# Cross-attention by block products: VectorE's sums woven, three more block products in fresh banks, one product of the result in blocks

## The chip, the cores and the metric

The kernel runs on one core of a Trainium2 chip. The metric is the time of one execution in device microseconds. Everything is in float32.

## The reference

For each of 8 batches, with x1 and x2 of 512 channels by 1024 places:

```
q = einsum("bcn,dc->bnd", x1, Wq) + bq            # 1024 x 64
k = einsum("bcn,dc->bdn", x2, Wk) + bk[:, None]   # 64 x 1024
v = einsum("bcn,dc->bdn", x2, Wv) + bv[:, None]   # 512 x 1024
attn = softmax(einsum("bnd,bdm->bnm", q, k), axis=2)
out  = einsum("bcm,bnm->bcn", v, attn) + x1
```

The kernel doesn't form v. It computes y = x2 times the transposed attention first (512 x 1024 by 1024 x 1024), and then the result as Wv times y, plus bv and x1.

## The kernel before

**Two large products, each by seven smaller ones.** Both y = x2 * e (e: the exponentials of the scores) and result = Wv * y are cut into 2 x 2 blocks and computed by a scheme of seven products in place of eight. `MULT` names for each product 1 to 7 its left and right operand and the bank in which it accumulates. Left operands are blocks 11, 12, 21, 22 and the sums S1 to S4; right operands blocks 11 to 22 and T1 to T4. The sums are made by VectorE (`left_sums`, `right_sums`, `sum_y`), by ScalarE, or by DMAs that accumulate (`add_11`, `sum_t3`, `sum_t4`). "Product 5 of y" and "product 7 of the result" below are these products; in the code the stages are "y" (`first`) and "o" (`second`).

**Blocks within a product.** A product of y is 256 x 512 by 512 x 512. Computed plainly (`multiply`, L365) it is eight matmuls of 128 x 128 by 128 x 512. It can be cut once more by the same scheme of seven: its left sums come from `inner_left`, its right sums from `inner_right`, and `inner_product` (L442) issues two matmuls of 256 columns per block product. Three small accumulators are used: `chain`, `third` and the banks of the product itself. ScalarE copies `chain` into the banks between the block products (L479), and VectorE adds `third` at the end (`complete`, L485). `multiply_seeded` does this in a fresh bank; `multiply_onto` does it on a bank that holds a sum already, with the parts that the chain gives in a tile `d` (L451), which VectorE adds later.

Before the change, products 1, 2, 7 and 3 of y are seeded in batches 1 to 7, product 4 goes onto bank c, product 5 goes onto bank a in batches 1 to 5 (`multiply_5`) and is plain in batches 6 and 7, and product 6 is plain. All seven products of the result are plain.

**Banks.** PSUM has eight banks of 512 columns: a0, a1, c0, c1 and two double ones (`sc`). The scores of one half (four tiles) use `sc` for three tiles and a pair of the others for one: c in half 0, a in half 1 (`scores_and`). `chain` and `third` take `sc` too.

**Order.** The instructions of each engine stand in the order in which the code emits them (`tc.manual_schedule`). `period(s, n, nn, nnn)` emits one batch s together with work for the next ones: the scores of batch n in halves 0 and 1, maxima (`fold`, `highest`), exponentials (`lower` on VectorE, `exponential` on ScalarE), sums of the exponentials (`total`), queries and keys of nn, and the loads of nnn. A batch runs on TensorE in this order: products 1, 2, 6 of y, scores of half 0, queries, products 5, 7, 3, scores of half 1, keys, product 4; then products 1, 6, 2, 5, 7, 3, 4 of the result. Batch 0 has an order of its own. In the last batch product 3 of the result comes last, and `evict_o("12")` writes out its halves.

**Names in the rows.** `yT L542` is `evict_t3`, `y L556` is `evict_y`, `y L547` is `scale_y`, `e L293` is `lower`, `e L297` the exponential, `max L248` and `sum L248` are folds, `aI L418` the left sums of blocks, `eI... L431, L434, L435` the right sums, `uy L524` and `d L531` the additions of `multiply_4` and `multiply_5`, `o`, `uo`, `x_in_x_dram L579 to L612` the eviction of the result. `den<-row` spreads a half's shares (one over the sum) over the partitions.

Of the kernel before, what the change touches and what calls it, by code (L numbers as in the profile page):

```python
# [15 lines left out]
def kernel(  # L16
# [195 lines left out]
    def scores(s, h, i, bank=None):  # L212
# [19 lines left out]
        def copy():  # L232
            if bank:
                for g in range(2):
                    nc.scalar.copy(e[:, g, i, :], ps[g])
            else:
                nc.scalar.copy(e[:, :, i, :], whole)  # L237
# [4 lines left out]
    def fold(s, h, i, kind, op):  # L242

        e = s.e[h]
        if i == 1:
            s.mx[h] = sb.tile([P, 2, H], F32, tag="fold", name=f"{kind}_{s.b}_{h}", bufs=2)
        f = s.mx[h]
        nc.vector.tensor_tensor(f, e[:, :, 0, :] if i == 1 else f, e[:, :, i, :], op)  # L248

# [44 lines left out]

    def exponential(s, h, i):
        e = s.e[h][:, :, i, :]
        nc.scalar.activation(e, e, AF.Exp)  # L297
# [39 lines left out]
    def sum_e(s, *ks, of=(0, 2)):  # L337
        for i in of:
            part = {n: v[:, i : i + 2, :] for n, v in s.t.items()}
            for k in ks:  # L340
                right_sums(part, k)

    def sum_y(s, k):
# [5 lines left out]
        else:  # L349
            nc.vector.tensor_tensor(y[k], y["22" if k == "T1" else "21"], y["T2"], ALU.subtract)  # L350

# [13 lines left out]
    def multiply(s, stage, i, left, right, n_k, last=False, hook=None):  # L365
# [4 lines left out]
        if stage == "o" and i == 2:  # L370
            bank, opens = "p", False
        for j in range(2):
# [22 lines left out]
    def multiply_o1(s):  # L395

        for j in range(2):
# [5 lines left out]
            s.bank["a", j] = a = ps_a.tile([P, H], F32, tag=f"a{j}", name=f"ps_oa{j}_{s.b}_1")  # L403
# [8 lines left out]
    def inner_left(s, i, x, tag):  # L412

        v = {f"{p + 1}{q + 1}": x[:, ts(q, MH // 2), ts(p, P)] for p in range(2) for q in range(2)}
        sums = sb.tile([P, 4, MH // 2, P], F32, tag=tag, name=f"aI{i}_{s.b}")
        for z, (k, x, y, op) in enumerate(LEFT):
            v[k] = sums[:, z]
            nc.vector.tensor_tensor(v[k], v[x], v[y], op)  # L418
        s.inner[i] = v

    def inner_right(s, i, x, *tags):

        v = {
            f"{q + 1}{r + 1}": x[:, ts(q, MH // 2), ts(r, H // 2)] for q in range(2) for r in range(2)
        }
        last = 4 // len(tags)
        shape = [P, last, MH // 2, H // 2]
# [5 lines left out]
        )  # L433
        nc.vector.tensor_tensor(t2, both[:, 0], v["22"], ALU.subtract)  # L434
        nc.vector.tensor_tensor(t4, v["21"], t2, ALU.add)  # L435
        s.inner[i, "t"] = v | {"T1": both[:, 0], "T3": both[:, 1], "T2": t2, "T4": t4}

    def inner_product(s, i, z, ps, opens, *copies):

        ka, kb, _, _ = MULT[z]  # L440
        for k in range(MH // 2):
# [5 lines left out]
                stop=z in (2, 3, 4) and k == MH // 2 - 1,  # L447
# [11 lines left out]
    def multiply_seeded(s, i, v_tag, hooks={}):  # L459

        bank = MULT[i][2]
        b0, b1 = (
            ps_a.tile([P, H], F32, tag=f"{bank}{j}", name=f"ps_y{bank}{j}_{s.b}_{i}") for j in range(2)
        )
        s.bank[bank, 0], s.bank[bank, 1] = b0, b1
        chain, third = inner_parts(s, i)
        v = sb.tile([P, 2, H], F32, tag=v_tag, name=f"v{i}_{s.b}")[:, 0, left]
        for z, ps, opens, out, of in (
            (1, chain, True, b0[:, left], chain),
            (7, third, True, v, third),  # L470
            (6, chain, False, b1[:, left], chain),
            (2, b0[:, left], False, None, None),
            (5, chain, False, b0[:, right], chain),
            (4, b1[:, left], False, b1[:, right], chain),
            (3, b0[:, right], False, None, None),
        ):
# [3 lines left out]
            if z in hooks:  # L480
                hooks[z]()

# [37 lines left out]
    def multiply_4(s, hooks={}):  # L520

        d, complete = multiply_onto(s, 4, "u5" if s.b < B - 1 else "a21", "r", hooks)
# [3 lines left out]
    def multiply_5(s, hooks):  # L526

        d, complete = multiply_onto(s, 5, "u5", "r", hooks)
        complete()
        for j in range(2):  # L530
            nc.vector.tensor_tensor(d[:, j, :], s.bank["a", j], d[:, j, :], ALU.add)  # L531
        s.tmp[5] = d
# [6 lines left out]
    def evict_t3(s):  # L539
        s.y["T3"] = y = sb.tile([P, 2, H], F32, tag="y12", name=f"yT3_{s.b}")  # L540
        for j in range(2):
            nc.vector.tensor_tensor(y[:, j, :], s.bank["a", j], s.tmp[7][:, j, :], ALU.add)  # L542
# [24 lines left out]
    def evict_o(s, k):  # L567


        bank, add = RESULT[k] if k != "11" else ("p", None)  # L570
        r, h = int(k[0]) - 1, int(k[1]) - 1
# [192 lines left out]
    def period(s, n, nn, nnn):  # L764
# [4 lines left out]
        def first(i):  # L769
            multiply(s, "y", i, s.a, s.t, MH)  # L770
# [19 lines left out]
        def scores_0():  # L790
            then = scores_and(n, 0, 1, "c", next_queries if nn else nothing)
# [14 lines left out]
        if n is None:  # L806
            load_x(s, x1)
# [33 lines left out]
        else:  # L841
# [10 lines left out]
            if n:  # L852
                sum_t3(s, 0)
                sum_t3(s, 2)
            complete_2()
            evict_y(s, "11")
            if n is None:
                sum_e(s, "T3")
            sum_t4(s)
            first(6)  # L860
            inner_left(s, 7, s.a["S3"], "yT4")
            if five:
                inner_left(s, 5, s.a["S1"], "i2")
                inner_right(s, 5, s.t["T1"], "y21", "u1")
            sum_a(s, "S4")
            if n:
                evict_q = scores_0()
            spread(s, 0)
            shares(s, 1)
# [152 lines left out]
```

## Time and profile before

| | |
|---|---|
| median of 3 runs | 682.23 us (681.3 to 682.25) |
| span of the profiled execution, first to last instruction | 680.8 us |
| TensorE busy | 672.1 us (99%) |
| weight loads, beside the matmuls | 397.9 us (58%) |
| VectorE busy | 615.2 us (90%) |
| ScalarE busy | 336.9 us (49%) |
| GpSimd busy | 218.5 us (32%) |
| DMA | 131.09 MB, 193 GB/s on the mean |
| batch 2, from 205.23 to 287.25 us | TensorE busy 82.02 of 82.02 us |

The page gives no time of the profiled execution beside its span; the three times lie 0.5 to 1.45 us above that span. A busy TensorE is one whose modelled matmul times touch each other. Rows of a timeline give the start in us from the span's start, the time in us, engine, line, operation, what is written from what, the count, and in brackets the idle time ahead with what ended it.

### The profile page before, as it was taken

What the parts mean: (1) busy time and instruction counts of PE and PEld (TensorE: products, weight loads), DVE (VectorE), ACT (ScalarE), POOL (GpSimd) and SP (SyncE); (2) the same over time, 40 slices, a digit from 0 to 9 for tenths busy, and PEclk for the clock granted to TensorE, in tenths of its full rate; (3) what the DMA queues carried; (4) which work ended last, traced back from release to release, by engine and by line L of the source; (5) the groups of instructions that cost most, each with busy time, mean ns of one, the idle gap of its engine ahead of it and who ended that gap; (6) DMA issues with size and microseconds to landing.
All of it is one profiled execution on the core that took longest, in us unless ns stands there. A gap on an engine that the chain in (4) does not pass through costs nothing.

```text
span 680.8 us, 7209 instructions
## 1 busy us (share of the span) xinstructions
PE 672.1 (99%) x2420; PEld 397.9 (58%) x2420; DVE 615.2 (90%) x763; ACT 336.9 (49%) x564; POOL 218.5 (32%) x182
## 2 busy tenths in 40 slices
PE   8999999999999999999999999999999999999997
PEld 5333554757547565566656576464854747556763
DVE  1999998899999999999999998999989979999884
ACT  2734266365554564544644637446475356553320
POOL 0124215251153502643125421344213451154100
PEclk9999999999999999999999999999999999999999
DMA  9656658967798759969499693996947985489503
GB/s 300 271 191 241 155 212 139 240 138 246 180 249 221 154 202 253 214 185 245 123 297 199 174 264 116 280 212 160 277 89 174 222 194 110 92 146 268 144 13 110
DMA packets 50772, 131.09 MB, mean 193 GB/s; under 512 B 5552, under 2 KB 7856, under 8 KB 50736
## 3 DMA queue, kind: packets, MB, share of 16 engines
q0 software_dynamic: 22464, 54.60, 44.7%
q1 hardware_dynamic: 27984, 75.64, 30.8%
q10 hardware_dynamic: 288, 0.39, 0.2%
q8 instruction: 19, 0.31, 0.2%
q14 instruction: 17, 0.14, 0.1%
HBM read 87.30 MB, written 16.81 MB: 153 GB/s over the span
## 4 chain that ended last, share of the span: by engine, by line
PE 84%; DVE 6%; DMA 5%; issue 2%; ACT 1%; SPq 1%; POOL 1%; DVEq 0%; POOLq 0%; ACTq 0%
PE ps_ya L380 11%; PE ps_oa L380 11%; PE ps_yc L442 8%; PE ps_oc L380 7%; PE ps_ya L442 6%; PE ps_s L228 5%; PE ps_o L400 4%; PE ps_o L380 4%; PE ps_k L181 3%; PE ps_q L181 3%; PE ps_i4chain L442 3%; PE ps_i3chain L442 3%; PE ps_i7chain L442 2%; PE ps_i1chain L442 2%; PE ps_i2chain L442 2%
## 5 line engine op out<-in xcount | busy, mean ns | idle before, releaser
L263 POOL PARTITION_ALL_REDUCE den<-sum x16 | 52.6, 3285 | 97.4 <-DVE few L271 60.3
L258 POOL PARTITION_ALL_REDUCE top<-max x16 | 37.6, 2352 | 126.3 <-DVE max L252 75.7
L380 PE MATMUL ps_ya<-eT,aS 128*128 128x512 f32 x176 | 77.5, 594 | 0.0
L293 DVE TENSOR_TENSOR e<-e,top 128x1024 f32<-128x1024 f32 x60 | 69.9, 1218 | 0.0
L620 POOL DMA_DIRECT2D sum<-e x21 | 32.1, 1530 | 108.7 <-ACT sum L625 42.0
L297 ACT ACTIVATE e<-e 128x1024 f32<-128x1024 f32 x60 | 61.8, 1058 | 4.7 <-DVE e L293 4.0
L380 PE MATMUL ps_oa<-yT,w_S 128*128 128x512 f32 x128 | 57.5, 592 | 0.0
L380 PE MATMUL ps_oc<-yT,w 128*128 128x512 f32 x128 | 57.4, 592 | 0.0
L380 PEld LDWEIGHTS ps_ya<-eT,aS 128*128 128x128 f32 x176 | 33.2, 190 | 40.1 <-issue 37.9
L237 ACT COPY e<-ps_s 128x1024 f32<-128x1024 f32 x46 | 45.6, 1032 | 9.0 <-PE ps_s L228 8.8
L228 PE MATMUL ps_s<-q,k 64*128 64x512 f32 x188 | 47.9, 608 | 0.9 <-ACT q L647 0.8
L380 PEld LDWEIGHTS ps_oa<-yT,w_S 128*128 128x128 f32 x128 | 24.3, 190 | 30.6 <-issue 30.6
L380 PEld LDWEIGHTS ps_oc<-yT,w 128*128 128x128 f32 x128 | 24.3, 190 | 30.6 <-issue 29.2
L248 DVE TENSOR_TENSOR max<-max,e 128x1024 f32<-128x1024 f32 x30 | 36.7, 1225 | 2.2
L391 ACT COPY uo<-ps_oa 128x512 f32<-128x512 f32 x32 | 18.7, 586 | 34.9 <-PE ps_oa L380 34.9
L391 ACT COPY uy<-ps_ya 128x512 f32<-128x512 f32 x24 | 13.9, 588 | 36.8 <-PE ps_ya L380 36.8
L228 PEld LDWEIGHTS ps_s<-q,k 64*128 64x128 f32 x188 | 17.1, 186 | 24.5 <-issue 18.0
L479 ACT COPY ps_ya<-ps_i1chain 128x256 f32<-128x256 f32 x28 | 10.0, 357 | 42.2 <-PE ps_i1chain L442 38.7
L547 DVE TENSOR_TENSOR y<-y,den 128x1024 f32<-128x1024 f32 x24 | 29.3, 1221 | 0.3
L418 DVE TENSOR_TENSOR aI<-a 128x256 f32<-128x256 f32 x58 | 29.4, 547 | 0.0
L380 PE MATMUL ps_oa<-y,w_S 128*128 128x512 f32 (+1 forms) x68 | 28.8, 567 | 0.0
L400 PE MATMUL ps_o<-y,w 128*128 128x512 f32 x64 | 28.8, 592 | 0.0
(202 smaller groups left out, 1539.0 us busy)
## 6 DMA issues: line engine op xcount, KB each, us to landing
x_in_x_dram<-in_x_dram SPq DMA_DIRECT2D x60, 512.0 KB, 7.6
a<-in_x2T_dram SPq DMA_DIRECT2D x32, 512.0 KB, 10.1
sum<-e POOLq DMA_DIRECT2D x21, 512.0 KB, 10.1
aS<-in_x2T_dram POOLq DMA_DIRECT2D x14, 512.0 KB, 8.9
uo<-in_x_dram POOLq DMA_DIRECT2D x14, 512.0 KB, 9.9
r<-in_x_dram POOLq DMA_DIRECT2D x14, 512.0 KB, 12.2
out_dram<-r SPq DMA_DIRECT2D x14, 512.0 KB, 6.5
eT<-eT POOLq DMA_DIRECT2D x14, 512.0 KB, 10.1
```

Of the source, the lines that this page charges most:

```text
L181: nc.tensor.matmul(ps[r, :], w_sb[:, c, :], s.x[:, c, ts(h, H)], start=(c == 0), stop=(c == CT - 1),)
L228: nc.tensor.matmul(ps[g], s.k[r, ts(i, P)], s.q[r, ts(h, H)], start=True, stop=True)
L237: nc.scalar.copy(e[:, :, i, :], whole)
L248: nc.vector.tensor_tensor(f, e[:, :, 0, :] if i == 1 else f, e[:, :, i, :], op)
L258: nc.gpsimd.partition_all_reduce(s.top[h], s.mx[h][:, 0, :], P, ReduceOp.max)
L263: nc.gpsimd.partition_all_reduce(s.den[h], s.mx[h][:, 0, :], P, ReduceOp.add)
L293: nc.vector.tensor_tensor(e, e, top, ALU.subtract)
L297: nc.scalar.activation(e, e, AF.Exp)
L380: nc.tensor.matmul(ps[:, n], left[ka][:, k, ts(j, P)], right[kb][:, k, n], start=opens and k == 0, stop=i in (2, 3, 4) and k == n_k - 1, s ...
L391: nc.scalar.copy(s.tmp[i][:, j, :], ps)
L400: nc.tensor.matmul(ps, w["11"][:, k, ts(j, P)], s.y["11"][:, k, :], start=k == 0, stop=False, skip_group_check=True)
L442: nc.tensor.matmul(ps, s.inner[i][ka][:, k, :], s.inner[i, "t"][kb][:, k, :], start=opens and k == 0, stop=z in (2, 3, 4) and k == MH // 2 ...
```

## The change

- **Products 3, 4 and 5 of y in fresh banks.** In batches 1 to 7 product 3 is seeded in bank c, product 4 in bank c (a in the last batch), and product 5 in bank a. y22 is then product 5 plus u6 plus product 7, so `join_67` adds the copy of product 7 to that of product 6, and y22 and y21 are evicted with it. `multiply_5` goes; `multiply_4` stays for batch 0.
- **Product 5 in blocks in batches 6 and 7 too.**
- **Product 7 of the result in blocks**, batches 1 to 7 (`multiply_57`): seven block products of one matmul of 256 columns each, with pieces of products 5 and 3 between them, so that product 3 comes ahead of product 4. Its left sums are made once, in batch 0 (`left_values`); its right sums from T3 of y in each batch. In the last batch half of product 3 (`rest`) still comes last. `o_bank` swaps banks a and c in the last batch.
- **VectorE's sums woven**: `inner_left` and `inner_right` become streams, and `weave` takes an instruction of each in turn. Left sums of 7 with the folds of the sum, left and right sums of 5, right sums of 7 with left sums of 3, right sums of 3 with a `lower`, left and right sums of 4, right sums of 1 with left sums of 2, and others.
- **Order.** In batches 1 to 5 the maxima of half 1 come ahead of the completion of product 4, and the last part of half 0's sum (`add_tile(n, 0, 3)`) and S3's (`add_11`) ahead of product 1 of the result. In the last batch T3 is made by ScalarE and a DMA, and the shares' reciprocals come later. In batch 6 the scores of half 0 come between the two halves of product 6, and those of half 1 are copied in another order. The last batch's x1 is loaded in batch 6.

```diff
+    def join_67(s):
+        nc.vector.tensor_tensor(s.tmp[6], s.tmp[6], s.tmp[7], ALU.add)
...
     def sum_e(s, *ks):
+        order = [(k, i) for i in (0, 2) for k in ks]
+        for k, i in order if s.b == 0 else sorted(order):
+            right_sums({n: v[:, i : i + 2, :] for n, v in s.t.items()}, k)
...
+    def weave(*streams):
+        streams = list(streams)
+        while streams:
+            for stream in list(streams):
+                if next(stream, "end") == "end":
+                    streams.remove(stream)
...
+    def multiply_57(s):
+        s.inner["o7"] = inner_w["o7"]
+        on, fresh = o_bank(s, "a"), o_bank(s, "c")
...
+        chain, third = inner_parts(s, "o7")
...
+        plain(5, 0, 0, 1)
+        inner_product(s, "o7", 1, chain, True, b0[:, left])
+        inner_product(s, "o7", 7, third, True, v)
+        plain(5, 1, 0)
+        inner_product(s, "o7", 6, chain, False, b1[:, left])
+        inner_product(s, "o7", 2, b0[:, left], False)
+        plain(5, 1, 1)
+        inner_product(s, "o7", 5, chain, False, b0[:, right])
+        inner_product(s, "o7", 4, b1[:, left], False)
+        nc.scalar.copy(b1[:, right], chain)
+        plain(3, 0, 0)
+        inner_product(s, "o7", 3, b0[:, right], False)
+        plain(3, 0, 1)
+        if s.b < B - 1:
+            plain(3, 1, 0, 1)
...
     def evict_t3(s):
-            nc.vector.tensor_tensor(y[:, j, :], s.bank["a", j], s.tmp[7][:, j, :], ALU.add)
+            nc.vector.tensor_tensor(
+                y[:, j, :], s.bank["c" if s.b else "a", j], s.tmp[7][:, j, :], ALU.add
+            )
...
     def evict_y(s, k):
         bank, add = RESULT[k]
+        if s.b and k == "22" or s.b == B - 1 and k == "21":
+            bank, add = "a", 6
...
     def scores_0():
-            then = scores_and(n, 0, 1, "c", next_queries if nn else nothing)
+            then = scores_and(n, 0, 1 if nn else 2, "c", next_queries if nn else nothing)
+            if nn is None:
+                first(6, (1,))
...
-            for i in range(1, MH):
-                fold(s, 1, i, "sum", ALU.add)
-            total(s, 1)
-            invert(s, 0)
+            sums_5 = left_stream(s, 5, s.a["S1"], "i2"), right_stream(s, 5, s.t["T1"], "y21", "u1")
+            if n:
+                weave(folds(s, 1, "sum", ALU.add), left_stream(s, 7, s.a["S3"], "yT4"))
+                total(s, 1)
+                invert(s, 0)
+            else:
+                weave(folds(s, 1, "sum", ALU.add), left_stream(s, 7, s.a["S3"], "yT4"))
+                weave(*sums_5)
...
-            if five:
-                multiply_5(s, {6: evict_q})
+            complete_5 = multiply_seeded(
+                s, 5, "r", {6: evict_q} if five else {}, "a"
+            )
+            complete_5()
             if n is None:
-                sum_e(s, "T3")
...
+                shares(s, 1)
...
-            hooks = {2: lambda: copy_7(s, 0), 5: lambda: copy_7(s, 1)}
+            hooks = {7: lambda: copy_7(s, 1)}
...
-            complete_3 = multiply_seeded(s, 3, "r", hooks)
+            copy_7(s, 0)
+            if n:
+                lower(n, 0, 1)
+            complete_3 = multiply_seeded(s, 3, "r", hooks, "c")
...
+            join_67(s)
+            evict_y(s, "22")
...
+            if n:
+                for i in range(2, MH):
+                    lower(n, 0, i)
             complete_3()
             evict_t3(s)
...
+            if nn is None:
+                load_x(n, x1)
...
+        if five:
+            weave(folds(n, 1, "max", ALU.max))
...
-        multiply_4(s, hooks)
+        if s.b == 0:
+            multiply_4(s, hooks)
+        else:
+            complete_4 = multiply_seeded(s, 4, "r", hooks, "c" if n else "a")
+            if five:
+                highest(n, 1)
+            complete_4()
...
         evict_y(s, "21")
+        if n is None:
+            sum_y(s, "T1")
+        if five:
+            add_tile(n, 0, 3)
+            add_11(n, "S3")
         scale_y(s, "21")
...
+        if five:
+            weave(iter_t4(s), right_stream(s, "o7", s.y["T3"], "eT1"))
...
-        second(5)
+        if late:
+            complete_7, rest = multiply_57(s)
+        else:
+            second(5)
...
-            second(3)
+            if s.b == 0:
+                second(3)
             evict_o(s, "12")
             second(4)
             total(n, 0)
...
         else:
             second(4)
             evict_o(s, "21")
-            second(3)
+            rest()
             evict_o(s, "12")
```

More of the change, by code (lines that the diff above doesn't have):

```diff
@@ L248, in fold, with folds @@
         nc.vector.tensor_tensor(f, e[:, :, 0, :] if i == 1 else f, e[:, :, i, :], op)
+    def folds(s, h, kind, op):
+        for i in range(1, MH):
+            fold(s, h, i, kind, op)
+            yield
     def fold_halves(s, h, op):
```

232 lines of the change are left out of this document (147 added, 85 removed).

## The prediction

> **What bounds the kernel now.** I read the page first, then busy time by stretch, then the waits of TensorE, the chain in order of time, and each engine's timeline over batch 2, which stands for batches 2 to 5.
>
> ```profile
> span 680.8 us, 7209 instructions
> ...
> PE 672.1 (99%) x2420; PEld 397.9 (58%) x2420; DVE 615.2 (90%) x763; ACT 336.9 (49%) x564; POOL 218.5 (32%) x182
> ```
>
> ```profile
> core 0: us, PE busy (x) PEld busy (x) DVE busy (x) ACT busy (x) POOL busy (x), PEclk, DMA share, GB/s
> ...
> 205.23:287.25 82.02, 82.02 (x306) 50.52 (x305) 77.71 (x98) 43.83 (x74) 28.99 (x24) 1.00 0.84 209
> ...
> 533.40:609.80 76.40, 76.11 (x262) 46.03 (x261) 70.75 (x87) 41.49 (x68) 28.93 (x24) 1.00 0.69 146
> 609.80:680.80 71.00, 67.19 (x229) 43.01 (x227) 55.07 (x73) 18.71 (x41) 11.61 (x10) 1.00 0.50 137
> ```
>
> The first row of stretches is batch 2: TensorE is busy for all 82.02 us at clock 1.00. The other two are batches 6 and 7, where VectorE is idle for 5.65 and 15.9 us. TensorE's price list stands in the chain; each matmul leaves two records, so x16 is eight matmuls.
>
> ```profile
> 194.07 3.43 PE ps_oc L380 x8
> ...
> 205.23 0.86 PE ps_i1third L442 x4
> ...
> 216.46 6.87 PE ps_ya L380 x16
> ```
>
> A plain product of y is eight matmuls of 512 columns, 6.87 us; a plain product of the result four, 3.43; one block product of y is two of 256 columns, 0.86, so 0.43 each. Two rows of TensorE's timeline bracket product 3 of y and one half's scores in batch 2:
>
> ```profile
> 242.66 1.03 PE L442 MATMUL ps_i3chain<-e,aS 128*128 128x256 f32 x4
> ...
> 252.48 3.65 PE L181 MATMUL ps_k<-x_in_x_dram,wqk_sb 128*64 128x512 f32 x16
> ```
>
> A product of y in blocks is 7 x 0.863 = 6.04 us, so one half's scores take 252.48 - 242.66 - 6.04 = 3.8, and a projection 3.6. Batch 2 has six products of y in blocks (36.2), one plain (6.9), seven plain ones of the result (24.0), two sets of scores and two projections (14.8): 81.9 of its 82.02 us are matmul slots. TensorE has no slack there, and a matmul less is time less, unless a new wait comes.
>
> **The change part by part.** My sum goes against the span of 680.8. The three times shown lie 0.5 to 1.45 us above it; their median, 682.23, is 1.4 above, and I carry that over.
>
> *Product 7 of the result in blocks, batches 1 to 7.* Four matmuls of 512 columns become seven of 256: 3.43 - 7 x 0.43 = 0.41 us; seven times, 2.9 us.
>
> *Product 5 of y in blocks in batches 6 and 7* (1 to 5 had it): 6.87 - 7 x 0.863 = 0.83 us, twice, 1.7 us. VectorE gets some 4.3 us more of sums in each; the idle 5.65 and 15.9 us of those two rows cover it. Without that cover batch 6 alone would lose what its product saves.
>
> *Products 3, 4 and 5 in fresh banks.* TensorE does the same here. What goes is a wait:
>
> ```profile
> PE ps_sa L228 <- DVE yT L542: 0.9, 1, 0.9
> ...
> PE ps_i4third L442 <- ACT e L237: 0.3, 1, 0.3
> ```
>
> ```profile
> 158.92 1.03 PE L442 MATMUL ps_i3chain<-e,aS 128*128 128x256 f32 x4
> ...
> 167.94 1.29 PE L228 MATMUL ps_sa<-q,k 64*128 64x512 f32 x3 [0.89 <-DVE yT L542]
> ...
> 170.44 1.94 PE L181 MATMUL ps_k<-x_in_x_dram,wqk_sb 128*64 128x512 f32 x8
> ```
>
> From product 3 to the keys takes 170.44 - 158.92 = 11.52 us in batch 1 and 252.48 - 242.66 = 9.82 in batch 2. In batch 1 the scores' third tile needs bank a, which evict_t3 (L542) still reads. Now product 3 lies in c, and bank a holds product 5, which VectorE evicts (y22) ahead of evict_t3. So 1.7 us goes. The other wait in the view, 0.3 in batch 6, is for a copy of the scores; I leave it. Next late after the one that goes would be y22: by the walk below it is evicted 5.4 us after product 3's start, and the tile comes some 8 us after it (6.04 of product 3 and two tiles of scores).
>
> *The weaving.* VectorE is the next engine, so its spacing decides whether these savings stand.
>
> ```profile
> 216.12 2.49 DVE L248 TENSOR_TENSOR sum<-sum,e 128x1024 f32<-128x1024 f32 x2
> ...
> 245.24 3.49 DVE L293 TENSOR_TENSOR e<-e,top 128x1024 f32<-128x1024 f32 x3
> 250.44 0.75 DVE L418 TENSOR_TENSOR aI<-a 128x256 f32<-128x256 f32 x2
> ...
> 271.53 1.59 DVE L418 TENSOR_TENSOR aI<-a 128x256 f32<-128x256 f32 x2
> ```
>
> Three independent instructions of 1024 take 3.49 us: they start (3.49 - 1.22) / 2 = 1.13 apart. Two of which the second needs the first take 2.49, so 1.25 apart. Putting another stream's instruction in between saves about 0.12 us per dependence; the woven pairs break some twenty in a batch, 2.4 us. [...]
>
> ```profile
> L524 DVE TENSOR_TENSOR uy<-uy,d 128x1024 f32<-128x1024 f32 x8 | 10.5, 1314 | 0.3
> L485 DVE TENSOR_TENSOR ps_yc<-ps_yc,v 128x512 f32<-128x512 f32 x14 | 9.6, 684 | 0.7 <-ACT ps_yc L479 0.7
> L531 DVE TENSOR_TENSOR d<-ps_ya,d 128x512 f32<-128x512 f32 x10 | 6.4, 682 | 0.0
> L418 DVE TENSOR_TENSOR aI<-a,aI 128x256 f32<-128x256 f32 x58 | 24.6, 425 | 2.0
> ```
>
> Against it stand, per batch: right sums of result product 7 (one of 512, 0.69; two of 256, 0.85) and its completion (0.69) added, 2.2 us; the two L531 additions gone, 1.3; L524's 1.31 replaced by join_67, some 1.25. VectorE's net is 0.9 - 2.4, or 1.5 us less. The four left sums of the weights, once in batch 0, cost 1.6; VectorE waits for half 0's sum there anyway.
>
> *The new order around product 4, batches 1 to 5.* Half 1's maxima (three folds, one of halves, and their all-reduce on POOL) now stand ahead of product 4's completion on VectorE. Queued behind them are y21's eviction and scaling, and TensorE's product 2 of the result waits for that.
>
> ```profile
> 244.59 0.37 ACT L479 COPY v<-ps_i3third 128x256 f32<-128x256 f32 x1 [0.51 <-PE ps_i3third L442]
> ```
>
> ```profile
> 261.37 0.69 DVE L516 TENSOR_TENSOR d<-d,v 128x512 f32<-128x512 f32 x1 [0.87 <-ACT d L451]
> ...
> 263.42 1.29 DVE L556 TENSOR_TENSOR y<-ps_yc,uy 128x512 f32<-128x512 f32 x2
> 264.75 1.23 DVE L547 TENSOR_TENSOR y<-y,den 128x1024 f32<-128x1024 f32 x1
> ```
>
> ```profile
> 269.08 3.60 PE L380 MATMUL ps_o<-y,w 128*128 128x512 f32 x8
> ```
>
> The walk on batch 2's clock: product 7's second copy follows ScalarE's row at 244.59 and ends near 245.5. VectorE's join_67 waits for it. Then join 1.3, y22 1.2, two lowerings 2.3, product 3's completion 0.6, T3 1.2, the woven sums of 4 3.7, three scalings 3.4, T2 1.1, three folds 3.7, halves 0.6: 264.7, where the old completion stood at 261.37. Completion 0.6, y21 1.3, scaling 1.2: ready at 267.9, and product 2 starts at 269.08. 1.2 us are left, so I cost this at nothing. Each us beyond them costs up to 5 us over the five batches. A stretch as in the row at 271.53 (1.59 for 0.75, beside the maximum's all-reduce) would take 0.84. In return half 0's last sum starts earlier on POOL.
>
> *Product 7's blocks amid 5 and 3.* With one slab, a block lasts 0.43 us, so ScalarE's copies must be quick.
>
> ```profile
> 205.33 0.36 ACT L479 COPY ps_ya<-ps_i1chain 128x256 f32<-128x256 f32 x1 [3.66 <-PE ps_i1chain L442]
> ```
>
> That copy is for a block that, by the chain, ended at about 205.07: it starts 0.26 later and lasts 0.36, 0.62 in all. In the new order a block and a piece of product 5 or 3 (0.43 + 0.86 = 1.29 us) lie between a block and whoever needs its copy. 0.6 us spare: zero, at worst 0.3 for each of three waits.
>
> *The end.* The last batch's product 3 moves its first half ahead of product 4; only its second half (1.7 us) follows it now.
>
> ```profile
> 673.38 3.61 PE L380 MATMUL ps_oa<-y,w_S 128*128 128x512 f32 x12
> ```
>
> ```profile
> 673.59 0.75 DVE L597 SCALAR_TENSOR_TENSOR x_in_x_dram<-ps_oc,bv_sb,x_in_x_dram 128x512 f32<-128x512 f32 x1 [0.82 <-PE ps_oc L380]
> 674.25 1.28 DVE L601 TENSOR_TENSOR x_in_x_dram<-x_in_x_dram,uo 128x512 f32<-128x512 f32 x2
> 675.45 0.74 DVE L589 SCALAR_TENSOR_TENSOR x_in_x_dram<-ps_oa,bv_sb,x_in_x_dram 128x512 f32<-128x512 f32 x1
> 677.03 0.88 DVE L589 SCALAR_TENSOR_TENSOR x_in_x_dram<-ps_oa,bv_sb,x_in_x_dram 128x256 f32<-128x256 f32 x2 [0.83 <-PE ps_oa L380]
> ```
>
> VectorE works 0.66 + 1.20 + 0.67 + 0.88 = 3.4 us from product 4's last matmul on. It had 3.43 us of matmuls beside it and ended 1.1 after TensorE; with 1.72 beside it, it ends at 0.2 + 3.4 - 1.7 = 1.9. Cost 0.8 us (0 to 1.3).
>
> *The last batch's shares.* Their reciprocals move behind the sums of product 7, and T3 to ScalarE and POOL.
>
> ```profile
> 639.11 0.54 POOL L278 DMA_DIRECT2D den<-row  x1 [4.00 <-DMA row<-few]
> ```
>
> ```profile
> 649.40 1.22 DVE L547 TENSOR_TENSOR yT<-yT,den 128x1024 f32<-128x1024 f32 x1
> ```
>
> ```profile
> den<-row POOLq DMA_DIRECT2D x16, 256.0 KB, 4.9
> ```
>
> Issued at 639.11, landing 4.9 later, used at 649.40: 5.4 us spare. The move takes an estimated 4.5 to 6 of it. Cost 0 to 1, I take 0.2. x1 loaded a batch ahead moves four loads past SP's others; in batch 6 the DMA share is 0.69, so nothing.
>
> Sum: -2.9 - 1.7 - 1.7 + 0.8 + 0.2 = -5.3. Span 675.5, time **676.9 us**.
>
> **The rivals.** *VectorE sets the pace (slower).* The place is product 2 of the result, waiting for y21. It decides from 1.2 us of lateness on: at 2.3 the gain of 5.3 is gone (1.1 in each of five batches), and from 2.6 on the kernel is slower than before. With two stretches of 0.84 (the maximum's all-reduce and the scaling, then the fold), product 7's completion, for which its second copy waits, later than the walk by the lowering of 1.13 that stands ahead of it, and weaving worth nothing in the sums of 4 (0.5) it is 3.3 late, and five batches lose 2.1 each, 10.5 us: 687.4. For it: 90% busy, and a row of 77.71 us in 82. Against it: the walk. The Trainium skill ("Perfetto Trace Analysis", section "Identifying the Most-Contended Engine") will not take matmul busy time as a measure, but weight-load time: 58% here, which would name VectorE. By that view the 0.4 us taken off TensorE in a batch would bring nothing, and the 0.9 that VectorE gains before weaving would lengthen it. Batch 2's slots, 81.9 of 82.02 us, speak against that.
>
> *The blocks of product 7 wait for their copies.* 0.3 x 3 x 7 = 6.3 us would eat the gain: 683, or, if only two of them wait, about 681. For it: ScalarE serves other copies there. Against it: 0.6 us spare each.
>
> *No new cost at the end and in batch 7 (faster still):* 675.9; with batch 6's 0.3 us ahead of product 4, and what it delays behind it, gone too, 675.2. Its scores are copied in another order now, half a tile less ahead of the copy that is waited for.
>
> **How the numbers follow.** The forecast's case has 0.55 (675.9 to 678.5), the one without costs 0.12, product 7's copies 0.12, VectorE 0.21: 0.05 of it late by less than 2.2 us and so faster or even, 0.16 by more. No change means within 0.2%, 1.4 us, which a measurement of this kernel can tell. Faster 0.76 (0.55, 0.12, half of the copies' 0.12, and 0.03), same 0.08, slower 0.16. The range reaches from 675.2 to 682.2; the slower cases lie above.
>
> **What would show it.** Right: matmuls of 256 columns in the result stage, no wait on L542's successor, 81.6 us per steady batch, product 3 to keys 9.8 us in batch 1. Wrong: TensorE idle ahead of product 2 of the result with VectorE as releaser, or between product 7's blocks with ScalarE; a steady batch of 82 us or more.

## The result, and the profile after

The changed kernel takes 678.14 us (median of 4 runs, 677.96 to 679.12), the kernel before 682.24 (4 runs, 681.30 to 682.44). The ratio is 0.9945, with a 95% interval from 0.9931 to 0.9959: 4.1 us faster, where 5.3 were forecast. The profiled run took 678.22, of which the span is 676.0; that of before was 680.8.

The page of the kernel after, its first rows:

```profile
span 676.0 us, 7484 instructions
...
PE 667.7 (99%) x2486; PEld 409.2 (61%) x2486; DVE 611.0 (90%) x799; ACT 352.1 (52%) x607; POOL 214.5 (32%) x184
```

TensorE has 66 records more, which are 33 matmuls at two records each, and 4.4 us less of work; VectorE has 36 instructions more and 4.2 us less. Busy time of each engine by stretch, for batches 2, 6 and 7, each from its product 1 of y to the next:

```profile
core 0: us, PE busy (x) PEld busy (x) DVE busy (x) ACT busy (x) POOL busy (x), PEclk, DMA share, GB/s
201.68:283.26 81.58, 81.58 (x311) 51.51 (x310) 75.47 (x101) 45.67 (x79) 28.10 (x26) 1.00 0.84 209
528.00:603.52 75.52, 75.21 (x279) 49.32 (x278) 74.27 (x99) 43.53 (x76) 27.79 (x25) 1.00 0.75 165
603.52:676.00 72.48, 67.49 (x251) 46.97 (x249) 59.85 (x86) 22.89 (x51) 15.48 (x14) 0.99 0.52 125
```

TensorE's timeline in the kernel before, where product 1 of y begins in batches 6 and 7 (the prediction's rows of these batches begin about 1 us later):

```profile
532.41 1.03 PE L442 MATMUL ps_i1chain<-e,a 128*128 128x256 f32 x4
...
608.83 1.03 PE L442 MATMUL ps_i1chain<-e,a 128*128 128x256 f32 x4
```

Batch 2 (and 3, 4 and 5 alike) is still full on TensorE and 0.4 to 0.6 us shorter. Batch 6 is 0.9 shorter; batch 7 is 0.5 *longer* than from its product 1 in the kernel before (608.83 to 680.8, 71.97). By stretch the span's 4.8 us are: head 0.36, batch 1 2.17, batches 2 to 5 1.88, batch 6 0.90, batch 7 -0.51. The head's 0.36 can't be told from chance: in the runs here product 1 of batch 1 begins anywhere from 119.2 to 120.6 us.

TensorE's waits, all but those of the first batch's start, and TensorE's timeline in batch 1 (start, duration, engine, line):

```profile
PE ps_ya L399 <- ACT e L294: 0.3, 1, 0.3
PE ps_i4chain L480 <- DVE aI L447: 0.2, 1, 0.2
```

```profile
158.56 1.03 PE L480 MATMUL ps_i3chain<-e,aS 128*128 128x256 f32 x4
...
166.52 1.02 PE L228 MATMUL ps_sa<-q,k 64*128 64x512 f32 x4
...
168.33 3.65 PE L181 MATMUL ps_k<-x_in_x_dram,wqk_sb 128*64 128x512 f32 x16
```

The wait for bank a is gone: product 3 to the keys takes 9.77 us. The timelines of VectorE and of TensorE in batch 2, where y21 is scaled and product 2 of the result follows, then product 7 in blocks:

```profile
264.14 1.23 DVE L647 TENSOR_TENSOR y<-y,den 128x1024 f32<-128x1024 f32 x1
```

```profile
266.51 3.60 PE L399 MATMUL ps_o<-y,w 128*128 128x512 f32 x8
...
271.66 0.59 PE L480 MATMUL ps_io7chain<-yT,w 128*128 128x256 f32 x2
...
273.38 0.59 PE L480 MATMUL ps_io7chain<-eIo7eT,w_I 128*128 128x256 f32 x2
...
275.10 0.59 PE L480 MATMUL ps_io7chain<-eIo7eT,w_I 128*128 128x256 f32 x2
```

y21 is ready at 265.37, 1.14 us ahead of product 2. The blocks whose copies are needed stand 1.72 apart each time, which is the sum of the matmuls between them (four times 0.43): none waits for ScalarE.

### The profile page after: what moved, and what is told of

Its sections match the earlier page's. It is cut to its first block, busy times and chain, and to the rows that moved or that the text cites. A ratio compares the mean times of both kernels' runs of the same rounds, so it can differ in the third digit from the quotient of the medians.

```text
span 676.0 us, 7484 instructions
## 1 busy us (share of the span) xinstructions
PE 667.7 (99%) x2486; PEld 409.2 (61%) x2486; DVE 611.0 (90%) x799; ACT 352.1 (52%) x607; POOL 214.5 (32%) x184
## 4 chain that ended last, share of the span: by engine, by line
PE 92%; DMA 3%; DVE 2%; SPq 1%; ACT 0%; issue 0%; DVEq 0%
PE ps_yc L480 10%; PE ps_ya L399 10%; PE ps_ya L480 6%; PE ps_oa L521 6%; PE ps_s L228 6%; PE ps_oa L399 5%; PE ps_oc L399 5%; PE ps_o L399 4%; PE ps_o L419 4%; PE ps_q L181 4%; PE ps_k L181 3%; PE ps_i4chain L480 3%; PE ps_i5chain L480 3%; PE ps_i3chain L480 3%; PE ps_i7chain L480 3%; PE ps_i1chain L480 3%
## 5 line engine op out<-in xcount | busy, mean ns | idle before, releaser
L399 PE MATMUL ps_ya<-eT,aS 128*128 128x512 f32 x144 | 63.7, 594 | 0.0
L264 POOL PARTITION_ALL_REDUCE top<-max x16 | 31.5, 1970 | 83.3 <-DVE max L258 44.5
L284 POOL DMA_DIRECT2D den<-row x16 | 9.0, 560 | 69.9 <-DMA row<-few 69.9
L719 POOL DMA_DIRECT2D r<-in_x_dram x14 | 27.8, 1982 | 4.0 <-ACT r L710 4.0
L399 PE MATMUL ps_oa<-yT,w_S 128*128 128x512 f32 x64 | 28.8, 592 | 0.0
L419 PE MATMUL ps_o<-y,w 128*128 128x512 f32 x64 | 28.8, 592 | 0.0
L399 PE MATMUL ps_o<-y,w 128*128 128x512 f32 x64 | 28.8, 592 | 0.0
L399 PE MATMUL ps_oc<-yT,w 128*128 128x512 f32 x64 | 28.8, 592 | 0.0
L181 PE MATMUL ps_k<-x_in_x_dram,wqk_sb 128*64 128x512 f32 x112 | 26.0, 600 | 0.6 <-DMA x_in_x_dram<-in_x_dram 0.6
L447 DVE TENSOR_TENSOR aI<-a,aI 128x256 f32<-128x256 f32 x58 | 25.1, 432 | 1.1
L181 PE MATMUL ps_q<-x_in_x_dram,wqk_sb 128*64 128x512 f32 x112 | 25.6, 598 | 0.0
```

Source lines behind the costliest of these rows:

```text
L181: nc.tensor.matmul(ps[r, :], w_sb[:, c, :], s.x[:, c, ts(h, H)], start=(c == 0), stop=(c == CT - 1),)
L264: nc.gpsimd.partition_all_reduce(s.top[h], s.mx[h][:, 0, :], P, ReduceOp.max)
L399: nc.tensor.matmul(ps[:, n], left[ka][:, k, ts(j, P)], right[kb][:, k, n], start=opens and k == 0, stop=i in (2, 3, 4) and k == n_k - 1, s ...
L419: nc.tensor.matmul(ps, w["11"][:, k, ts(j, P)], s.y["11"][:, k, :], start=k == 0, stop=False, skip_group_check=True)
```

## The experiments

Times are medians; each ratio is to the kernel before, run on the same chip, with its 95% interval. The edits are to the changed kernel, where nothing else is said, and `...` marks what is left out. Differences in us are taken from the changed kernel's 678.14, which was measured in another round; the kernel before itself came to 681.8 to 682.2 in the rounds of the experiments and to 682.24 beside the changed kernel, so some 0.4 us of such a difference can be the round.

### Weaving

```diff
-        while streams:
-            for stream in list(streams):
-                if next(stream, "end") == "end":
-                    streams.remove(stream)
+        for stream in streams:
+            for step in stream:
+                pass
```

> Each stream of VectorE runs to its end before the next begins; all else is as in the changed kernel (678.1 us). Theory (TensorE's matmul slots set the time; y21 has 1.14 us to spare ahead of product 2 of the result in batches 1 to 5): VectorE loses some 0.1 us per dependence, 1.5 to 2.5 a batch, but only the sums of product 4 lie ahead of y21 (0.5 us), so batches 1 to 5 stay at 81.6 us and the whole comes to 678.1 to 679.5. Rival (VectorE sets the pace): seven batches lose some 2 us each, 690 or more. Rival (the spacing of VectorE's instructions doesn't depend on their order): VectorE's rows stand as close as before and the time is 678.1.

681.79 us, ratio 0.9998 (0.9989 to 1.0008): 3.65 slower than the changed kernel, nearly its whole gain. Busy time by stretch, of batches 2, 6 and 7:

```profile
201.77:283.35 81.58, 81.58 (x311) 51.51 (x310) 77.52 (x101) 45.65 (x79) 28.08 (x26) 1.00 0.85 209
528.09:607.69 79.60, 77.65 (x279) 50.79 (x278) 77.06 (x99) 43.62 (x76) 27.44 (x25) 0.98 0.73 158
607.69:681.20 73.51, 67.87 (x251) 46.87 (x249) 60.78 (x86) 22.97 (x51) 15.47 (x14) 1.00 0.50 122
```

Batch 2 is to the hundredth as long as in the changed kernel, with 2.05 us more on VectorE: hidden, as the theory had it, and no pace of VectorE there. But batch 6 loses 4.1 us in this run and batch 7 1.0, where the theory had next to nothing. TensorE's timeline in product 4 of y of batch 6 shows where most of it goes:

```profile
577.13 1.10 PE L478 MATMUL ps_i4third<-eI4eT,aI 128*128 128x256 f32 x4 [1.90 <-DVE eI4eT L460]
578.07 1.84 PE L478 MATMUL ps_i4chain<-eI4eT,aI 128*128 128x256 f32 x4
579.70 1.91 PE L478 MATMUL ps_yc<-eT,a 128*128 128x256 f32 x4
```

All the left sums of 4 now come ahead of the right ones, and the first right sum is late. The two rows behind the wait last 1.8 to 1.9 us, where such a row lasts 1.03: the clock, see the last section. The fall is not in every run: this one was the slowest of ten (683.45 us), the three runs of 682.6 us or more have a mean granted clock of 0.997, and the other seven, of 682.2 us or less, 0.999 or 1.000.

### Product 7 of the result, and product 5 of y, plain again

```diff
-            complete_7, rest = multiply_57(s)
+            second(5)
...
-            complete_7()
+            second(7)
```

> Product 7 of the result as four plain matmuls of 512 columns in batches 1 to 7, its sums and its completion left out; the order at the end stays. Theory (slots): 7 x 0.41 = 2.9 us come back, less up to 0.7 at the end, where VectorE no longer completes product 7: 680.3 to 681.0. Rival (the blocks wait for ScalarE's copies and bring nothing): 678.1.

679.90 us, ratio 0.9970 (0.9957 to 0.9983): 1.76 slower. The stretches of batches 2, 6 and 7:

```profile
202.13:284.12 81.99, 81.99 (x305) 50.37 (x304) 73.88 (x97) 44.00 (x74) 29.00 (x24) 1.00 0.83 208
530.10:605.71 75.61, 75.30 (x274) 48.16 (x273) 73.19 (x96) 42.23 (x71) 27.97 (x24) 1.00 0.74 167
605.71:678.00 72.29, 67.33 (x245) 46.10 (x243) 56.03 (x79) 21.34 (x46) 13.30 (x12) 0.99 0.48 121
```

The blocks bring exactly 0.41 in batch 2, as priced, but only 0.09 in batch 6, and in batch 7 they cost 0.19. Both theories missed: the saving is real, and in the last two batches other waits take it back, which the section on the prediction follows up.

Product 5 of y, plain in batches 6 and 7 alone:

```diff
+            if five:
                 complete_5 = multiply_seeded(s, 5, "r", {6: evict_q} if five else {}, "a")
                 complete_5()
+            else:
+                plain_5()
```

> Product 5 of y plain (eight matmuls of 512 columns, in its fresh bank) in batches 6 and 7 alone, its VectorE sums there left out. Theory (slots): 2 x 0.83 = 1.7 us come back, less some 0.3 in batch 7, where the sums of product 7 come late behind those of 5: 679.4 to 679.8. Rival (VectorE sets the pace of the last two batches, so that its 4 us of sums cost what the blocks save): 678.1 or less.

680.34 us, ratio 0.9975 (0.9965 to 0.9986): 2.2 slower, more than the 1.7 of the slots. Batch 6 takes 76.35 us, 0.83 more, as priced. Batch 7 takes 73.76, 1.28 more: the wait in product 7 of y goes (0.32), but the plain product waits itself, as TensorE's timeline says, since it begins in a bank that a copy of product 6 still reads:

```profile
624.20 7.13 PE L885 MATMUL ps_ya<-eT,aS 128*128 128x512 f32 x16 [0.55 <-ACT uy L410]
```

### How late y21 may be

```diff
             weave(folds(n, 1, "max", ALU.max))
+            for _ in range(3):
+                fold(n, 1, MH - 1, "max", ALU.max)
```

> In batches 1 to 5 the last fold of half 1's maxima is made three more times (a maximum with the same tile, so the values stay): some 3 x 1.25 = 3.75 us more on VectorE ahead of y21. Theory (y21 has 1.14 us to spare, and from there on TensorE pays us for us): 5 x 2.6 = 13 us, 691.2, with TensorE waiting ahead of product 2 of the result. Rival (VectorE sets the pace already): 5 x 3.75 = 18.8 us, 696.9. Rival (there is more cover than the trace shows): 678.1.

697.50 us, ratio 1.0223 (1.0200 to 1.0246), more than either theory. TensorE's waits:

```profile
PE ps_o L399 <- DVE y L647: 12.6, 5, 2.5
```

```profile
356.21 5.40 PE L399 MATMUL ps_o<-y,w 128*128 128x512 f32 x8 [2.53 <-DVE y L647]
```

The wait is the one foretold, five times 2.5 us, and three of the batches are 2.8 longer. The two others are 4.5 longer: there product 2, behind the wait, lasted 5.40 us and not 3.60 (the row is batch 3's, from TensorE's timeline), at a granted clock of 0.68. That the time is near the second theory's 696.9 is chance: its 3.75 us a batch are in no batch. The profiled run, 695.39, was the fastest of four; the others, up to 699.27, may have had more of these falls. So with two folds:

> As the run with three more folds, with two. Theory: y21 is 2.5 - 1.14 = 1.4 us late plus 0.2 of restart, 5 x 1.6 = 8 us, 686, if TensorE's clock stays at 1.00 behind a wait of that length; with 1.7 us for each time that it falls behind the wait, as it did in two batches of five behind 2.5 us: 689.5 for two.

686.21 us, ratio 1.0064 (1.0048 to 1.0080), and the waits:

```profile
PE ps_o L399 <- DVE y L647: 6.7, 5, 1.7
```

8.1 us slower, 8.0 foretold; all five products 2 behind these waits kept their clock. The margin of 1.14 us and the price of one us per us beyond it hold (1.5 us more in four of the batches, 1.9 in one).

### The bank of the third score tile

```diff
-                scores_and(n, 1, 2, "a", nothing)
+                scores_and(n, 1, 2, "c" if late else "a", nothing)
```

> In batches 1 to 5 the third score tile of half 1 goes into bank c, where product 3 now lies, and not into bank a: the wait that the kernel before had in batch 1, put back into the new order. Theory: the tile's matmuls come at 248.09 in batch 2 and would wait for the eviction of T3, whose row ends at 249.56: 1.5 us in each of five batches, 7.3 in all, 685.4. Rival (the tile would find something else to wait for anyway, or the eviction is early enough): 678.1.

686.39 us, ratio 1.0065 (1.0050 to 1.0080): 8.3 slower. TensorE's timeline in batch 2:

```profile
247.18 1.99 PE L228 MATMUL ps_s<-q,k 64*128 64x512 f32 x8
249.93 1.29 PE L228 MATMUL ps_sc<-q,k 64*128 64x512 f32 x3 [0.76 <-DVE yT L640]
```

The wait is back in all five batches. Four of them are 1.62 us longer and one 1.82; the trace books 0.76 of it, ahead of the tile's first matmuls. It is the wait that the kernel before had in batch 1; what removes it is that product 3 and the tile lie in different banks.

### Where the maxima stand

```diff
-        if five:
-            weave(folds(n, 1, "max", ALU.max))
...
-            if five:
-                highest(n, 1)
             complete_4()
...
             add_tile(n, 0, 3)
-            add_11(n, "S3")
         scale_y(s, "21")
...
             weave(iter_t4(s), right_stream(s, "o7", s.y["T3"], "eT1"))
+            weave(folds(n, 1, "max", ALU.max))
+            highest(n, 1)
+            add_11(n, "S3")
```

S3's accumulating DMA (`add_11`) moves back with the maxima, which the expectation doesn't say.

> In batches 1 to 5 half 1's maxima and their all-reduce stand behind the scaling of y21 again, as in the kernel before; all else as in the changed kernel. Theory (their place is hidden either way while y21 keeps its 1.14 us): batches 1 to 5 stay at 81.6 us, 678.1, within 0.7. Rival (their early place is what brings the gain, through half 0's last sum and the exponentials of half 1): 1 us or more per batch, 683 or more.

687.34 us, ratio 1.0079 (1.0063 to 1.0094): the theory falls by 9 us. Batches 1 to 3 take 0.6 more each, batch 4 6.2 and batch 6 1.1, and the releaser is one that I had not thought of. POOL's and TensorE's timelines in batch 4:

```profile
440.22 1.17 POOL L723 DMA_DIRECT2D sum<-e  x1 [9.02 <-ACT ps_oc L489]
440.99 2.18 POOL L264 PARTITION_ALL_REDUCE top<-max  x1
```

```profile
449.14 5.40 PE L399 MATMUL ps_oc<-yT,w 128*128 128x512 f32 x8 [4.24 <-DVE uo L715]
```

Product 4 of the result waits for the eviction of o22 (L715), which VectorE has queued behind four lowerings, which wait for the maxima's all-reduce, which stands on POOL behind the last accumulation of half 0's sum. That accumulation waited for the one ahead of it, issued at 430.01 and landed 9.4 us later (the row names a copy of ScalarE's in its place), and I had left it at its new, early place. To tell the queue from the maxima themselves, on top of the edit above:

```diff
-            add_tile(n, 0, 3)
         scale_y(s, "21")
...
         evict_o(s, "11")
         if n:
-            if not five:
-                add_tile(n, 0, 3)
+            add_tile(n, 0, 3)
```

> Half 1's maxima stand behind the scaling of y21 as in the run with late maxima (687.3), and half 0's last accumulation too goes back to where the kernel before had it, behind the eviction of o11, so that on POOL the maxima's all-reduce no longer stands behind it. Theory (there the all-reduce waited on POOL's queue behind an accumulation that itself waited for the one before to land; VectorE's lowerings, the completion of product 7 of the result and the eviction of o22 were queued behind it, and product 4 of the result waits for that eviction): product 4 comes on time again, 678.1 to 679.5. Rival (the late maxima alone cost that): 682 or more.

681.78 us, ratio 0.9994 (0.9985 to 1.0003), between the two. Product 4 is on time again and batches 1 to 5 take 81.6 us: POOL's queue was the cause of the loss there, and S3's accumulation, still late here, was not. Batch 6, though, takes 77.68 us, 2.2 more than in the changed kernel; the profiled run was the fastest of ten (680.64 us), so it doesn't show all of the median's 3.6. VectorE's timeline at its start and TensorE's:

```profile
532.18 0.69 DVE L258 TENSOR_TENSOR sum<-sum 128x512 f32<-128x512 f32 x1 [0.99 <-DMA sum<-e]
```

```profile
547.09 1.72 PE L228 MATMUL ps_sc<-q,k 64*128 64x512 f32 x4 [1.37 <-DVE y L658]
```

Half 0's sum reaches VectorE 2.2 us later in its batch than in the changed kernel: 0.99 is the wait for the accumulation, and the rest is VectorE's queue, in which the lowerings behind the late maxima run later. The eviction of y11 is behind it, and the scores' tile needs y11's bank. No run has the maxima early and the accumulation late, so what each place is worth by itself stays open.

### The end, and the last two batches

```diff
+        if n is None:
+            o = s.x[:, 2:4, ts(0, H)]
+            nc.vector.tensor_tensor(o, o, s.tmp[6], ALU.add)
         if late:
             complete_7()
...
             second(4)
+            evict_o(s, "12", (0,))
             evict_o(s, "21")
             rest()
-            evict_o(s, "12")
+            evict_o(s, "12", (1,))
```

> Only the last batch's end is changed: the sum of product 6 is added to x1 while VectorE is idle, the first half of product 3's result is evicted ahead of product 4's, and each half of product 4's result takes one instruction and not two. VectorE then ends about 0.7 us behind TensorE and not 1.9. Theory (the end is set by VectorE's rows behind the last matmuls): 1.1 to 1.2 us less, 677.0. Rival (the queue of the output transfers sets the end): 678.1.

676.93 us, ratio 0.9926 (0.9909 to 0.9942): 1.2 faster than the changed kernel, and the lowest time here. VectorE's last rows, in the changed kernel and then with the new end:

```profile
669.33 0.75 DVE L700 SCALAR_TENSOR_TENSOR x_in_x_dram<-ps_oa,bv_sb,x_in_x_dram 128x512 f32<-128x512 f32 x1 [0.96 <-PE ps_oa L399]
670.00 1.28 DVE L704 TENSOR_TENSOR x_in_x_dram<-x_in_x_dram,uo 128x512 f32<-128x512 f32 x2
671.20 1.52 DVE L692 SCALAR_TENSOR_TENSOR x_in_x_dram<-ps_oc,bv_sb,x_in_x_dram 128x512 f32<-128x512 f32 x3
```

```profile
669.40 0.75 DVE L710 SCALAR_TENSOR_TENSOR x_in_x_dram<-ps_oa,bv_sb,x_in_x_dram 128x512 f32<-128x512 f32 x1 [0.61 <-PE ps_oa L399]
671.13 0.88 DVE L694 SCALAR_TENSOR_TENSOR x_in_x_dram<-ps_oc,bv_sb,x_in_x_dram 128x256 f32<-128x256 f32 x2 [0.97 <-PE ps_oc L521]
```

VectorE ends at 672.72 and at 672.01, with spans of 676.0 and 674.9: 0.7 of the 1.1 us lies in VectorE's rows, and 0.4 behind the last of them, where no row says why.

Four changes of order on top of that, in batches 6 and 7:

```diff
+            if n and nn is None:
+                copy_t4(s)
             sum_t3(s, 0)
...
+                inner_right(s, 7, s.t["T3"], "yT1", "yT2")
                 sum_a(s, "S4")
-                weave(right_stream(s, 7, s.t["T3"], "yT1", "yT2"), left_stream(s, 3, s.a["S4"], "aI3"))
+                inner_left(s, 3, s.a["S4"], "aI3")
...
-            if n:
+            if nn:
                 for i in range(2, MH):
                     lower(n, 0, i)
...
-                third(0)
                 scores(n, 1, 3)()
-                third(1)
+                third()
...
+            if nn is None:
+                for i in range(2, MH):
+                    lower(n, 0, i)
```

> The end as in the run before it, and three more changes of order in the last two batches. Batch 6: ScalarE's copies for T4 stand ahead of its negations, so that the scores between the halves of product 6 find their copies sooner (0.3 us); the third score tile of half 1 is copied whole, behind the fourth, and two lowerings stand behind the sums of product 4 (0.4 to 0.5 us ahead of and in product 4). Batch 7: the right sums of product 7 stand ahead of the sum S4 and the left sums of 3 (0.3 us). Theory (each is a wait of TensorE in the trace, and TensorE has nothing else to wait for): 1.15 + 0.3 + 0.45 + 0.3 = 2.2 us less than the changed kernel, 675.9. Rival (each wait only passes to the next one): 677.0, that of the end alone.

677.60 us, ratio 0.9935 (0.9920 to 0.9950): nothing gained on the end alone. Batch 6 gained 0.32 up to product 1 of the result and lost 0.34 ahead of product 4 of the result; batch 7 gained 0.32 in product 7 of y and lost 0.78 in product 4. A second attempt at the two new waits, as an edit to that run's kernel:

```diff
-                inner_right(s, 7, s.t["T3"], "yT1", "yT2")
+                weave(left_stream(s, 4, s.a["22"], "a11"), right_stream(s, 7, s.t["T3"], "yT1", "yT2"))
...
-            if n is None:
-                inner_left(s, 4, s.a["22"], "a12")
...
-            for i in range(2 if s.b == 0 else 0, MH):
+            for i in range(2 if s.b == 0 else 0, MH if nn else MH - 1):
                 exponentials(n, 1, i)
...
+        if n and nn is None:
+            exponentials(n, 1, MH - 1)
```

> The end and batch 6's copies as in the run with four changes of order (there batch 6 gained 0.32 us up to product 1 of the result and gave it back ahead of product 4 of the result; batch 7 gained 0.32 in product 7 and lost 0.78 in product 4 of y). Two more changes: in batch 6 the last lowering of half 1 stands behind the eviction of o22; in batch 7 the left sums of product 4 are woven into the right sums of 7, where VectorE had waited 0.55 us for a transfer. Theory (VectorE's order, not its amount of work, makes these waits): batch 6 75.2 us, batch 7 to the start of product 1 of the result 43.1 us, 0.65 less in all than the kernel with the new end alone (676.93): 676.3. Rival (VectorE is full in both batches, a wait that is taken away comes back): 676.9 or more.

677.95 us, ratio 0.9936 (0.9922 to 0.9950). Batch 6 came to 75.19 us, as the theory had it, but batch 7 lost more than that: up to product 1 of the result it took 44.9 us, not 43.1. The lowering put off in batch 6 now runs ahead of VectorE's sums for batch 7, which begin 0.6 us later against batch 7's product 1 than in the changed kernel, and products 5 and 3 of y take 0.9 and 0.8 us longer. Product 5's wait comes ahead of the newly woven sums; which of the two changes costs product 3 its 0.8 isn't separated. In both tries a wait that was taken away came back a few products on; the rival holds.

## Why the prediction was right, and where it was off

**The size: 1.2 us short, and most of it outside the span.** The span came to 676.0, where the sum had 675.5. The other 0.8 is the 1.4 that the prediction carried over from span to time. It set a median against the span of another run: run by run the time lies 1.7 to 1.8 us above the span in the kernel before (in the rounds of the experiments), and 2.2 to 2.3 in the changed kernel. Why the changed kernel spends 0.45 us more outside its span no run here shows. Within the span, batches 1 to 5 gained 0.3 more than forecast, batches 6 and 7 lost 0.34 and 0.75 against it, and the head's 0.36 made up for some of that, which was luck.

**The sign and the bound: right.** TensorE's slots set batches 1 to 5. Product 7 of the result saves 0.41 us a batch there (81.58 us, forecast 81.6), and without its blocks the 0.41 comes back. Product 3 to the keys takes 9.77 (9.8).

**The weaving: right in size, half right in worth.** In the sums of 4 of batch 2 it saves 0.5 us (3.67 against 4.17, from the first sum to the scaling behind them); in the whole batch 2.05, where I had 2.4. The run without it has 2.05 us more of VectorE in a batch and is 3.65 us slower in all. The section "The DRAIN you can't avoid" of the Trainium skill's page "VectorE: DVE Perf Modes" says that an operation doesn't start before the pipe of the one ahead is empty, and also that one that is "not held" starts earlier. The prediction's rows agree with the latter for independent instructions: they last 1.22 us and start 1.13 apart. I called the weaving hidden: true of batches 1 to 5, not of the last two.

**The place of the maxima: right cost, wrong reason.** The walk to y21 was exact (1.2 us to spare, 1.14 measured, and the runs with more folds confirm the price). But I treated the early maxima as a burden only. With them ahead, half 0's last accumulation can go early without standing before their all-reduce on POOL, and VectorE has half 0's sum in time in batch 6, the one batch that the old place of both made clearly longer. The old place of both costs 3.6 us, the accumulation's new place with the maxima's old one 9. The chain behind it, from the all-reduce over the lowerings and the eviction of o22 to product 4 of the result, was in none of my parts.

**Batch 6: the step that failed is product 7's 0.41 there, one of the "seven times, 2.9 us".** Forecast 1.24 less, measured 0.90. The sums of 5 were covered in this batch, as the prediction said: with product 5 plain it takes the full 0.83 more. Product 7's blocks brought 0.09 and not 0.41. The rest lies in half 0's scores, which now stand between the halves of product 6, an order that the prediction didn't cost. TensorE's, VectorE's and ScalarE's timelines, and in the last fence ScalarE's with product 7 of the result plain:

```profile
543.62 1.99 PE L228 MATMUL ps_s<-q,k 64*128 64x512 f32 x8
545.44 1.08 PE L228 MATMUL ps_sc<-q,k 64*128 64x512 f32 x4
546.51 1.13 PE L228 MATMUL ps_s<-q,k 64*128 64x512 f32 x4
547.57 3.70 PE L399 MATMUL ps_ya<-eT,aS 128*128 128x512 f32 x8
```

```profile
540.88 1.21 DVE L248 TENSOR_TENSOR sum<-sum,e 128x1024 f32<-128x1024 f32 x1
```

```profile
542.12 1.06 ACT L340 ACTIVATE e<-e 128x1024 f32<-128x1024 f32 x1 [0.88 <-DVE sum L248]
543.09 1.98 ACT L333 COPY eT<-e 128x1024 f32<-128x1024 f32 x2
544.97 0.58 ACT L410 COPY uy<-ps_ya 128x512 f32<-128x512 f32 x1
545.45 1.93 ACT L237 COPY e<-ps_s 128x1024 f32<-128x1024 f32 x2
```

```profile
542.26 2.02 ACT L340 ACTIVATE e<-e 128x1024 f32<-128x1024 f32 x2
```

The scores take 4.0 us (3.6 before). The first tile is ready at about 544.5, its copy starts at 545.45, and the fourth tile needs that buffer. The copy is late because it stands behind the copies for T4, these behind a negation (L340), and the negation waits 0.88 us for VectorE's last fold of half 1's sum, which reads what it overwrites. That fold comes 12.88 us after product 1 began, and 11.43 with product 7 plain, where VectorE has no sums and no completion of product 7 ahead of it; there ScalarE's two negations run without a gap and the scores take 3.6. The run that puts the copies ahead of the negations takes 3.7. With product 5 plain the wait stays. A stretch's idle time is no cover for a sum that another engine needs by a moment.

**Batch 7: the term for the end, 0.8 (0 to 1.3), was 1.4; and product 7 of y lost 0.3.** VectorE ended 1.9 us behind TensorE, as forecast, which is 0.8 more than before. The rest: 0.25 in small gaps ahead of TensorE's last two products, whose releaser the trace doesn't name, and 0.39 more from VectorE's end to that of the span (3.28 against 2.89), whose cause isn't shown either. The gaps are absent with product 7 of the result plain. The new end took 1.2 of the 1.4 back. Product 7 of y begins at 628.52, and VectorE's sum for its second block starts only at 628.20:

```profile
626.58 1.70 DVE L108 SCALAR_TENSOR_TENSOR aS<-a,aS 128x1024 f32<-128x1024 f32 x1
628.20 1.21 DVE L462 TENSOR_TENSOR eI7yT<-e 128x1024 f32<-128x1024 f32 x1
```

It stands behind the sums of 5, which are new there, and product 7 takes 6.37 us and not 6.04. Here the step "the idle 5.65 and 15.9 us of those two rows cover it" failed: with product 5 plain product 7 takes 6.05, and also with product 7 of the result plain, where VectorE comes earlier into the batch, so it takes both to make it late. The 0.2 for the shares was not spent: the spread is issued at 641.00 and used at 645.68, in time.

**The rivals.** VectorE's case, product 2 of the result waiting for y21, did not happen, but a milder form of it happened in the last two batches and ate 0.7 us: VectorE late for product 7 of y in batch 7, and, through ScalarE, for the scores in batch 6. The section "Identifying the Most-Contended Engine" of the Trainium skill's page "Perfetto Trace Analysis" would by its weight-load time (61% here, against VectorE's 90%) name VectorE throughout; its other measure, the share of the peak arithmetic, isn't worked out here. Batches 1 to 5 disagree (2.05 us more on it cost nothing), while batches 6 and 7 bear out that it counts there. The case of product 7's blocks waiting did not happen.

## What to carry to other kernels

An engine's idle time in a stretch is a sum of gaps; whether it covers new work is read from when each result is needed, and a kernel's last batches, with fewer matmuls beside the same sums, have another bound than its steady ones. When work moves earlier on one engine, follow it through every queue it enters (here POOL's, then VectorE's) to the instruction that waits at the end of the chain. At the end, count what stands behind the last matmul: moving three VectorE instructions ahead of it brought 1.2 us, as much as three steady batches of saved matmuls.

## What the runs showed of the hardware

A wait of TensorE can cost more than its length. Behind waits of 2.5 us the granted clock fell in two batches of five, behind 4.2 us once, behind 1.9 us once; behind six waits of 1.3 to 1.7 us it did not. The stretch of product 2 behind such a wait with three folds more, then the one behind the wait without weaving and one us out of that (columns as above, each of its own run):

```profile
356.20:361.50 5.30, 5.29 (x9) 2.28 (x10) 5.16 (x10) 0.69 (x1) 3.12 (x3) 0.68 0.83 250
```

```profile
577.10:581.40 4.30, 4.27 (x12) 3.45 (x13) 4.27 (x5) 2.65 (x4) 1.20 (x1) 0.62 0.00 0
...
579.00:580.00 1.00, 1.00 (x4) 0.81 (x3) 1.00 (x2) 0.60 (x2) 0.12 (x1) 0.50 0.00 0
```

Within the stretch the clock is 0.50. A mean of 0.68 over 5.3 us and of 0.62 over 4.3 are then each about 3.3 us at half, some 1.7 us lost. The Trainium skill ("TensorE: Matmul & The Clock Gate", section "Part 1: The HAM clock gate (the "warmup" mystery)") has a free-running window of about 3.4 us and half the clock after an idle one: the length and the half agree with these rows, and a free-running window would explain why equal waits differ, though no run here shows that. The page's section "HAM oscillation — how this bites in real kernels" gives as the abstract rule that no idle gap be above some 3.4 us; here that is too mild, since waits of 1.9 and 2.5 us did it.
